# Graph attention on one core: query-key products added by plain products with the identity instead of by transposes and a selection matrix

## The chip, the core and the metric

The kernel runs on one core of a Trainium2 chip. A core has five engines that run side by side, each with its own queue of instructions that it takes in order: TensorE (PE, matrix products; its weight loads are shown apart as PEld), VectorE (DVE), ScalarE (ACT), GpSimd (POOL, which here mostly issues gathers) and SyncE (SP, which issues DMAs). Matrix products are written into PSUM, a small memory of eight banks of 512 float32 values on each of 128 partitions[...]. The metric is the time of one execution on the device in microseconds.

## What is computed

The input x is 8 batches of 2048 nodes with 256 features, and a 2048 x 2048 adjacency matrix that is nearly empty. Layer 0 is attention with 4 heads of 64 features, whose softmax runs over each chunk of 256 columns by itself; layer 1 is a graph attention over neighbours; each is followed by a residual and a layer norm. The part that matters here is the product of queries and keys:

```python
scores = jnp.einsum('bhnd,bhjcd->bhnjc', q, kc) / jnp.sqrt(jnp.asarray(Dh, dtype=q.dtype))
scores = jnp.clip(scores, -10.0, 10.0)
scores = jnp.where(mask == 0, jnp.asarray(-10.0, scores.dtype), scores)
attn = jax.nn.softmax(scores, axis=-1)
ctx = jnp.einsum('bhnjc,bhjcd->bhnd', attn, vc)
```

## The kernel before

The adjacency matrix has only a few neighbours in each row, so the kernel works on lists. `edge_lists` takes from each row the columns that are set, sorts the nodes by their number of neighbours and cuts them into 16 tiles of 128 nodes. All nodes of tile t are given the same number of slots, `CAPS[t]`, from 24 down to 5, together 164. A slot holds one neighbour of each of the tile's nodes.

The batches go in four groups of two (g = 0 to 3), so a row of keys has 512 values and there are 8 pairs of batch and head (`GH`). One step of layer 0 is one tile of one group, which makes 64 steps. The sequence is written out at the end of the function (L762 to L858): 32 steps of groups 0 and 1, then 32 steps of groups 2 and 3 with 16 steps of layer 1 (for the first four batches) put between them, then 16 steps of layer 1 alone. A scheduler may still move an instruction past others of its engine where no data forbids it, so that neighbouring steps mix on each engine.

In a step of layer 0 these functions run, in this order in the program:

- `fetch`, one step ahead (L802): `gather` (L483) has POOL fetch, slot by slot, the rows of keys and values of the neighbours into the tiles `u` of a ring. A tile `u` holds a unit, which is two slots (one where the number is odd and the unit is the last). It is released when TensorE has read it for the last time.
- `scores0` (L531): the products of queries and keys, told below.
- `rows1` (L653) for the step before the last and `finish0` (L629) for the last one: output projection, residual, layer norms and the table rows for layer 1.
- `tables` (L354), while g + 1 < 4: keys, values and queries of the next group, written to DRAM. So 48 of the 64 steps build tables.
- `softmax0` (L586): the clip, the exponential and the sums by chunk.
- `context0` (L610): VectorE (L501) or ScalarE (L507) multiplies the values by the weights, and TensorE adds the slots up (`summed`, L509) by transposes with the identity that accumulate in PSUM.

In `scores0` the 64 features of a head are split into 8 parts of 8: the columns of a row of keys are ordered (part j, batch and head, 8 features), 8 x 64 = 512. The first unit and the last third of the units are done by VectorE alone (`reduced`: multiply at L554, sum at L556). For the other units (`npe` - 1 of them: 8, 5, 5, 4, 4, 4, 4, 4, 4, 4, 3, 3, 3, 3, 2, 2 for the tiles, 62 in each group) VectorE only multiplies (`product`, L547), and writes the result over the keys of the unit before, sorted so that each part j has 128 columns, which are 2 slots x 8 pairs x 8 features. Then:

- TensorE transposes each of the 8 parts and adds them in PSUM (L566): the result in bank `pr` has the 128 columns on partitions and the 128 nodes along the row. Up to four units share the bank; there is one such bank.
- ScalarE copies the bank to `prT` in SBUF (L572, L574).
- TensorE multiplies each unit by `sel` (L576), a matrix of 128 x 16 that adds eight neighbouring partitions and so the last 8 features; the product has nodes on partitions again and is put in bank `tf`.
- In `softmax0` VectorE clips these scores on the way from `tf` to `sc` (L590) and those of the units that it summed itself (L593).

PSUM is full: `mf` 1 bank, `tk` 2, `acc` 2, `tf` 2, `pr` 1.

Of the kernel before, what the change touches and what calls it, by code (L numbers as in the profile page):

```python
# [9 lines left out]
F32 = mybir.dt.float32  # L10
# [4 lines left out]
ALU = mybir.AluOpType  # L15
AX = mybir.AxisListType

P = 128
H = 4
D = 64  # L20
DP = 8
NJ = D // DP
# [15 lines left out]
UNIT = 2  # L38
# [135 lines left out]
def sparse_path(ctx: ExitStack, tc: tile.TileContext, keep, x, adj, Wq, bq, Wk, bk, Wv, bv, Wo, bo, gamma, beta, W, a,  # L174
                out):
    nc = tc.nc
# [6 lines left out]
    GH = G * H  # L183
# [15 lines left out]
    const = ctx.enter_context(tc.tile_pool(name="const", bufs=1))  # L199
# [13 lines left out]
    def by_part(v):  # L213
        return v.rearrange("p (j h d) -> p h j d", h=H, d=DP)


    sel = const.tile([P, P // DP], F32, name="sel")
    nc.gpsimd.memset(sel, 1.0)
    nc.gpsimd.affine_select(out=sel, in_=sel, compare_op=ALU.is_ge, fill=0.0, base=0, pattern=[[-DP, P // DP]],
                            channel_multiplier=1)  # L220
    nc.gpsimd.affine_select(out=sel, in_=sel, compare_op=ALU.is_ge, fill=0.0, base=DP - 1, pattern=[[DP, P // DP]],
                            channel_multiplier=-1)
    biasT = const.tile([P, 3, KC], F32, name="biasT")

    def row(v):
# [6 lines left out]
    def bank(tag, bufs=2):  # L232

        return ps.tile([P, 512], F32, tag=tag, name=tag, bufs=bufs)
# [296 lines left out]
    def scores0(g, t):  # L531
        S = CAPS[t]
        qx, units = got0[g, t]
        q = qx[:, 0:GF]
        sc = small.tile([P, GH, S], F32, tag="sc", name="sc")

        npe = 1 + len(units) - len(units) // 3
        ps_sc = bank("tf")[:, 0:GH * S].rearrange("p (s e) -> p s e", e=GH)
        W8 = GH * DP
        qv = q.rearrange("p (k j w) -> p k j w", k=UNIT, w=W8).unsqueeze(3)  # L540

        def product(i):

            u, s0, n = units[i]
            room = units[i - 1][0][:, :, 0:GF]
            prod = room.rearrange("p k (j w) -> p k j w", w=UNIT * W8)[:, :, :, 0:n * W8]
            nc.vector.tensor_tensor(prod.rearrange("p k j (s w) -> p k j s w", w=W8),  # L547
                                    u[:, :, 0:GF].rearrange("p s (k j w) -> p k j s w", k=UNIT, w=W8),
                                    qv.to_broadcast([P, UNIT, NJ // UNIT, n, W8]), op=ALU.mult)
            return prod  # L550

        def reduced(u, s0, n):
            prod = u[:, :, 0:GF].rearrange("p s (j w) -> p s j w", w=W8)
            nc.vector.tensor_tensor(prod, prod, q.rearrange("p (j w) -> p j w", w=W8).unsqueeze(1)  # L554
                                    .to_broadcast([P, n, NJ, W8]), op=ALU.mult)
            nc.vector.tensor_reduce(sc[:, :, s0:s0 + n].rearrange("p e s -> p s e"),  # L556
                                    prod.rearrange("p s j (e d) -> p s e j d", d=DP),
                                    axis=AX.XY, op=ALU.add)
        reduced(*units[0])
        for i in range(1, npe, 4):  # L560
            some = units[i:min(i + 4, npe)]
            pr = bank("pr", 1).rearrange("p (k r) -> p k r", r=P)
            for k, (u, s0, n) in enumerate(some):
                prod = product(i + k)
                for j in range(NJ):
                    nc.tensor.matmul(pr[0:n * W8, k, :], prod[:, j // (NJ // UNIT), j % (NJ // UNIT), :], ident, is_transpose=True,  # L566
                                     start=(j == 0), stop=(j == NJ - 1), skip_group_check=True)
            m = len(some)
            prT = work.tile([P, 4, P], F32, tag="prT", name="prT", bufs=1)
            full = m - 1 if some[-1][2] < UNIT else m  # L570
            if full:
                nc.scalar.copy(prT[:, 0:full, :], pr[:, 0:full, :])  # L572
            if full < m:
                nc.scalar.copy(prT[0:W8, full, :], pr[0:W8, full, :])  # L574
            for k, (u, s0, n) in enumerate(some):
                nc.tensor.matmul(ps_sc[:, s0:s0 + n, :], prT[0:n * W8, k, :], sel[0:n * W8, 0:n * GH],  # L576
                                 start=(s0 == UNIT), stop=(k == m - 1 and i + m == npe), skip_group_check=True)
        for unit in units[npe:]:
            reduced(*unit)
        st0[g, t] = ps_sc, sc, min(S, UNIT * npe)  # L580


    ebuf = const.tile([P, GH * TOP + 1], F32, name="ebuf")
# [2 lines left out]
    def softmax0(g, t):  # L586
        S = CAPS[t]
        n = GH * S
        ps_sc, sc, sp = st0.pop((g, t))
        nc.vector.tensor_scalar(sc[:, :, UNIT:sp], ps_sc[:, UNIT:sp, :].rearrange("p s e -> p e s"), -10.0, 10.0, op0=ALU.max,  # L590
                                op1=ALU.min)
        for some in [sc[:, :, 0:UNIT]] + ([sc[:, :, sp:]] if sp < S else []):
            nc.vector.tensor_scalar(some, some, -10.0, 10.0, op0=ALU.max, op1=ALU.min)  # L593
        e = ebuf[:, 0:n]
        ev = e.rearrange("p (e s) -> p e s", s=S)
        nc.scalar.activation(ev, sc, AF.Exp)
# [56 lines left out]
    def rows1(g, t):  # L653

        o = st0.pop((g, t))
        pt = transposed(o.rearrange("p b f -> p (b f)"), "tf", 2)
        xT = work.tile([P, G * KC, P], F32, tag="x1T", name="x1T", bufs=1)
        nc.scalar.copy(xT, pt)  # L658
        wh = work.tile([P, WW], F32, tag="whs", name="whs")
# [627 lines left out]
```

## Time and profile before

| what | value |
|---|---|
| median of 3 runs | 2385.73 us (2379.63 to 2388.16) |
| the profiled execution | 2397.55 us, of which the span of instructions 2395.8 us |
| mean granted TensorE clock | 0.885 of full speed |
| score products on TensorE (L566) | 1984 instructions, from 223.6 to 1933.8 us |
| copies to prT on ScalarE (L572, L574) | 96 |
| gathers of keys and values on POOL (L489) | 656, mean 1235 ns |
| DMA engines | 279 GB/s, software queue 60.1% of the 16 engines' span |

All details come from the profiled execution. An engine is busy while at least one of its instructions is under way; matrix products overlap in TensorE's pipeline, and their ends are modelled, so its busy share is higher than the share in which it takes up new work. A line such as L566 is a line of the kernel before. A wait is put down to the instruction whose end came last. PE and PEld are the product and the weight load of the same unit; each product has its load.

### The profile page before, as it was taken

What the parts mean: (1) busy time and instruction counts of PE and PEld (TensorE: products, weight loads), DVE (VectorE), ACT (ScalarE), POOL (GpSimd) and SP (SyncE); (2) the same over time, 40 slices, a digit from 0 to 9 for tenths busy, and PEclk for the clock granted to TensorE, in tenths of its full rate; (3) what the DMA queues carried; (4) which work ended last, traced back from release to release, by engine and by line L of the source; (5) the groups of instructions that cost most, each with busy time, mean ns of one, the idle gap of its engine ahead of it and who ended that gap; (6) DMA issues with size and microseconds to landing.
All of it is one profiled execution on the core that took longest, in us unless ns stands there. A gap on an engine that the chain in (4) does not pass through costs nothing. (4 is left out here: it accounts for less than half of the span.)

```text
span 2395.8 us, 38844 instructions
## 1 busy us (share of the span) xinstructions
PE 1900.4 (79%) x11946; PEld 1622.0 (68%) x11946; DVE 1833.5 (77%) x4099; ACT 1409.0 (59%) x5036; POOL 1505.0 (63%) x1230
## 2 busy tenths in 40 slices
PE   7686889889899898999988885888678786664764
PEld 5565677778778787777876774776566675554653
DVE  6864587877588988588988886887788887775775
ACT  4573455546566555655565665664356677665766
POOL 3125455672666676376668856774677685787883
PEclk9897899899999999999998997987878987877887
DMA  7737877795889798598879977896679896786884
GB/s 259 242 137 272 265 270 281 260 346 209 316 287 320 260 334 319 212 388 298 302 258 353 360 281 238 285 321 221 230 274 326 306 319 248 278 310 231 302 296 154
DMA packets 239982, 669.10 MB, mean 279 GB/s; under 512 B 43688, under 2 KB 70059, under 8 KB 237719
## 3 DMA queue, kind: packets, MB, share of 16 engines
q0 software_dynamic: 156800, 505.01, 60.1%
q1 hardware_dynamic: 79248, 151.55, 17.2%
q10 hardware_dynamic: 3718, 9.97, 1.3%
q8 instruction: 98, 1.61, 0.3%
q14 instruction: 118, 0.96, 0.1%
HBM read 612.79 MB, written 126.36 MB: 309 GB/s over the span
## 5 line engine op out<-in xcount | busy, mean ns | idle before, releaser
L489 POOL DMA_INDIRECT u<-kv_d,idx x656 | 810.2, 1235 | 436.4 <-PE acc L514 185.7
L514 PE MATMUL acc<-ident,u 128*128 128x128 f32 x5248 | 713.4, 291 | 157.0 <-DVE u L501 89.0
L514 PEld LDWEIGHTS acc<-ident,u 128*128 128x128 f32 x5248 | 637.5, 151 | 220.7 <-DVE u L501 133.2
L489 POOL DMA_INDIRECT u<-wh_d,idx x328 | 416.5, 1270 | 148.2 <-issue 76.4
L566 PE MATMUL pr<-ident,u 128*128 128x128 f32 (+1 forms) x1984 | 287.0, 295 | 78.7 <-DVE u L547 77.2
L501 DVE TENSOR_TENSOR u<-u,al 128x1024 f32<-128x1024 f32 x280 | 334.5, 1234 | 1.5
L566 PEld LDWEIGHTS pr<-ident,u 128*128 128x128 f32 (+1 forms) x1984 | 245.4, 151 | 110.8 <-DVE u L547 104.6
L547 DVE TENSOR_TENSOR u<-u,qx 128x1024 f32<-128x1024 f32 (+1 forms) x248 | 302.0, 1218 | 18.3 <-DMA u<-kv_d,idx 15.1
L501 DVE TENSOR_TENSOR u<-u,z 128x1024 f32<-128x1024 f32 x266 | 314.4, 1212 | 0.6
L507 ACT ACTIVATE u<-u,z 128x64 f32<-128x64 f32 x1008 | 262.0, 337 | 25.0 <-DVE z L700 17.1
L507 ACT ACTIVATE u<-u,al 128x64 f32<-128x64 f32 x800 | 209.1, 342 | 23.2 <-DVE al L607 22.3
L663 PE MATMUL mf<-wa,x1T 128*128 128x264 f32 x512 | 167.6, 455 | 23.1 <-ACT x1T L658 14.8
L351 POOL TENSOR_TENSOR xt<-xt,beta_r 128x1024 f32<-128x1024 f32 x32 | 77.1, 2410 | 143.1 <-PE tk L336 126.3
L385 PE MATMUL tk<-wq,xT 128*128 128x256 f32 x512 | 145.2, 397 | 24.4 <-ACT kvs L379 24.4
L451 ACT ACTIVATE nm<-sums 128x2 f32<-128x2 f32 (+1 forms) x160 | 32.4, 202 | 221.3 <-DVE sums L641 122.6
L372 PE MATMUL tk<-wkv,xT 128*128 128x256 f32 x512 | 151.7, 410 | 12.9 <-ACT xC L341 12.6
L635 PE MATMUL mf<-wo,cT 128*128 128x256 f32 x512 | 148.4, 415 | 6.3 <-ACT whs L666 5.3
L376 PE MATMUL tk<-wkv,xC 128*128 128x256 f32 x512 | 144.5, 399 | 0.0
L663 PEld LDWEIGHTS mf<-wa,x1T 128*128 128x128 f32 x512 | 101.7, 218 | 59.7 <-ACT x1T L658 23.6
L455 ACT ACTIVATE sq<-o,nm 128x256 bf16<-128x256 f32 x256 | 129.7, 507 | 5.3
L554 DVE TENSOR_TENSOR u<-u,qx 128x1024 f32<-128x1024 f32 (+1 forms) x96 | 116.0, 1214 | 16.6 <-DMA qx<-qx_d,node 7.1
L590 DVE TENSOR_SCALAR sc<-tf 128x64 f32<-128x64 f32 (+5 forms) x64 | 14.0, 218 | 138.2 <-PE tf L576 138.2
(168 smaller groups left out, 3254.0 us busy)
## 6 DMA issues: line engine op xcount, KB each, us to landing
kv_d<-kvs SPq DMA_DIRECT2D x48, 512.0 KB, 6.0
wh_d<-whs SPq DMA_DIRECT2D x64, 260.0 KB, 5.8
xt<-in_x_dram SPq DMA_DIRECT2D x64, 256.0 KB, 4.8
qx_d<-xt SPq DMA_DIRECT2D x32, 512.0 KB, 4.4
qx_d<-qs SPq DMA_DIRECT2D x64, 256.0 KB, 5.8
x_d<-o SPq DMA_DIRECT2D x64, 256.0 KB, 5.2
xr<-x_d SPq DMA_DIRECT2D x32, 512.0 KB, 4.9
u<-kv_d,idx POOLq DMA_INDIRECT x656, 6.5
```

The costliest lines, as they stand in the source:

```text
L372: nc.tensor.matmul(pm[:, 0:F], xT[:, b * KC + kc, rows], wkv[:, kc, 0:F], start=(kc == 0), stop=False, skip_group_check=True)
L376: nc.tensor.matmul(pm[:, F:], xC[:, b * KC + kc, rows], wkv[:, kc, F:], start=False, stop=(kc == KC - 1), skip_group_check=True)
L385: nc.tensor.matmul(qb, xT[:, b * KC + kc, rows], wq[:, kc, :], start=(b == 0 and kc == 0), stop=False, skip_group_check=True)
L455: nc.scalar.activation(sq, src[:, k, :], AF.Square, bias=nm[:, k:k + 1], accum_out=m2[:, k:k + 1])
L489: nc.gpsimd.indirect_dma_start(out=u[:, k, 0:width], out_offset=None, in_=table, in_offset=bass.IndirectOffsetOnAxis(ap=idx[:, t, s0 + k:s ...
L501: nc.vector.tensor_tensor(pv, pv, av, op=ALU.mult)
L507: nc.scalar.activation(pe, pe, AF.Copy, scale=al[:, e, s0 + k:s0 + k + 1])
L514: nc.tensor.matmul(acc[:, c, :], part[:, k, c * P:(c + 1) * P], ident, is_transpose=True, start=first and k == 0 and c == 0, stop=last and ...
L547: nc.vector.tensor_tensor(prod.rearrange("p k j (s w) -> p k j s w", w=W8), u[:, :, 0:GF].rearrange("p s (k j w) -> p k j s w", k=UNIT, w=W8),
L566: nc.tensor.matmul(pr[0:n * W8, k, :], prod[:, j // (NJ // UNIT), j % (NJ // UNIT), :], ident, is_transpose=True, start=(j == 0), stop=(j ...
L635: nc.tensor.matmul(po[:, b, :], cT[:, b * KC + kc, :], wo[:, kc, :], start=(b == 0 and kc == 0), stop=False, skip_group_check=True)
L663: nc.tensor.matmul(pw[:, 0:F + 2 * H], xT[:, b * KC + kc, :], wa[:, kc, :], start=(kc == 0), stop=(kc == KC - 1))
```

## The change

A plain product with the identity as the stationary matrix gives back the moving matrix; eight of them into the same place in PSUM add eight matrices without transposing them. The change does this with the eight parts of a unit: the nodes stay on partitions, and the 128 columns of a unit (slots, pairs, 8 features) lie along the row of the bank. Four units fill a bank of 512. What is left, the sum over the last 8 features, is done by VectorE in `softmax0`, by a reduction that reads the bank. The copies to `prT`, the products with `sel` and `sel` itself go. The clip is one instruction over all of a tile's scores. Bank `pr` gets two buffers, `tf` keeps one, which only `rows1` uses.

```diff
@@ -213,13 +213,6 @@
-    sel = const.tile([P, P // DP], F32, name="sel")
-    nc.gpsimd.memset(sel, 1.0)
...
@@ -535,7 +528,7 @@
-        ps_sc = bank("tf")[:, 0:GH * S].rearrange("p (s e) -> p s e", e=GH)
+        sums = []
@@ -559,25 +552,18 @@
-            pr = bank("pr", 1).rearrange("p (k r) -> p k r", r=P)
+            ns = sum(n for _, _, n in some)
+            pr = bank("pr")
             for k, (u, s0, n) in enumerate(some):
                 prod = product(i + k)
+                part = pr[:, k * UNIT * W8:(k * UNIT + n) * W8]
                 for j in range(NJ):
-                    nc.tensor.matmul(pr[0:n * W8, k, :], prod[:, j // (NJ // UNIT), j % (NJ // UNIT), :], ident, is_transpose=True,
-                                     start=(j == 0), stop=(j == NJ - 1), skip_group_check=True)
-            m = len(some)
-            prT = work.tile([P, 4, P], F32, tag="prT", name="prT", bufs=1)
-            full = m - 1 if some[-1][2] < UNIT else m
-            if full:
-                nc.scalar.copy(prT[:, 0:full, :], pr[:, 0:full, :])
-            if full < m:
-                nc.scalar.copy(prT[0:W8, full, :], pr[0:W8, full, :])
-            for k, (u, s0, n) in enumerate(some):
-                nc.tensor.matmul(ps_sc[:, s0:s0 + n, :], prT[0:n * W8, k, :], sel[0:n * W8, 0:n * GH],
-                                 start=(s0 == UNIT), stop=(k == m - 1 and i + m == npe), skip_group_check=True)
+                    nc.tensor.matmul(part, ident, prod[:, j // (NJ // UNIT), j % (NJ // UNIT), :], start=(k == 0 and j == 0),
+                                     stop=(k == len(some) - 1 and j == NJ - 1), skip_group_check=True)
+            sums.append((some[0][1], ns, pr))
         for unit in units[npe:]:
             reduced(*unit)
-        st0[g, t] = ps_sc, sc, min(S, UNIT * npe)
+        st0[g, t] = sc, sums
@@ -586,11 +572,11 @@
-        ps_sc, sc, sp = st0.pop((g, t))
-        nc.vector.tensor_scalar(sc[:, :, UNIT:sp], ps_sc[:, UNIT:sp, :].rearrange("p s e -> p e s"), -10.0, 10.0, op0=ALU.max,
-                                op1=ALU.min)
-        for some in [sc[:, :, 0:UNIT]] + ([sc[:, :, sp:]] if sp < S else []):
-            nc.vector.tensor_scalar(some, some, -10.0, 10.0, op0=ALU.max, op1=ALU.min)
+        sc, sums = st0.pop((g, t))
+        for s0, ns, pr in sums:
+            nc.vector.tensor_reduce(sc[:, :, s0:s0 + ns].rearrange("p e s -> p s e"),
+                                    pr[:, 0:ns * GH * DP].rearrange("p (s e d) -> p s e d", e=GH, d=DP), axis=AX.X, op=ALU.add)
+        nc.vector.tensor_scalar(sc, sc, -10.0, 10.0, op0=ALU.max, op1=ALU.min)
@@ -653,7 +639,7 @@
-        pt = transposed(o.rearrange("p b f -> p (b f)"), "tf", 2)
+        pt = transposed(o.rearrange("p b f -> p (b f)"), "tf", 1)
```

More of the change, by code (lines that the diff above doesn't have):

```diff
@@ L214, in by_part @@
         return v.rearrange("p (j h d) -> p h j d", h=H, d=DP)
-    sel = const.tile([P, P // DP], F32, name="sel")
-    nc.gpsimd.memset(sel, 1.0)
[L219 to L222, printed above, removed]
     biasT = const.tile([P, 3, KC], F32, name="biasT")
```

## The prediction

> **What bounds the kernel now.** I read the page first (busy shares, slices, chain), then the busy time by stage, the groups with their shapes kept apart, the table of waits, and TensorE's timeline at one place. The chain of waits that the page prints holds only the last scatter, 0.1% of the span, so it says nothing about the middle; the stages have to. The steps that the change touches run from 230 us (first score) to 1940 us (last one); what comes before (edge lists) and after (layer 1 alone) is left as it is.
>
> ```profile
> PE 1900.4 (79%) x11946; PEld 1622.0 (68%) x11946; DVE 1833.5 (77%) x4099; ACT 1409.0 (59%) x5036; POOL 1505.0 (63%) x1230
> ...
> 230.00:780.00 550.00, 488.83 (x3045) 416.96 (x3046) 419.04 (x822) 296.20 (x1124) 322.07 (x261) 0.92 0.82 286
> 780.00:1250.00 470.00, 424.88 (x2809) 365.38 (x2808) 383.63 (x757) 278.23 (x1065) 303.84 (x237) 0.97 0.83 298
> 1250.00:1600.00 350.00, 283.38 (x1871) 245.37 (x1869) 282.54 (x623) 216.80 (x803) 254.43 (x196) 0.89 0.86 305
> 1600.00:1940.00 340.00, 256.49 (x1588) 219.24 (x1587) 275.04 (x598) 183.83 (x664) 231.36 (x183) 0.82 0.80 277
> ```
>
> Columns of the stages: length, then busy time and count of PE, its weight loads, DVE, ACT, POOL, then granted clock, DMA share, GB/s. While tables are built (the first two rows) PE is busy 89 and 90% of the time, DVE 76 and 82%; ACT and POOL have room. Later DVE is first (81%), PE second. So the two engines to which this change gives work are the two fullest ones, and the one that it relieves, ACT, is not.
>
> ```profile
> L566 PE MATMUL pr<-ident,u 128*128 128x128 f32 x1824 | 267.4, 296 | 78.7 <-DVE u L547 77.2
> L372 PE MATMUL tk<-wkv,xT 128*128 128x256 f32 x512 | 151.7, 410 | 12.9 <-ACT xC L341 12.6 <-ACT kvs L379 0.2
> L576 PE MATMUL tf<-sel,prT 128*128 128x16 f32 x456 | 65.7, 270 | 32.2 <-ACT prT L572 31.4
> L556 DVE TENSOR_REDUCE sc<-u 128x16 f32<-128x1024 f32 x84 | 101.8, 1212 | 0.5
> L738 DVE SCALAR_TENSOR_TENSOR xr<-mf,xr 128x512 f32<-128x512 f32 x64 | 43.8, 684 | 21.5 <-ACT hT L737 9.9 <-DMA xr<-x_d 7.5 <-SPq L868 4.1
> L572 ACT COPY prT<-pr 128x512 f32<-128x512 f32 x36 | 20.9, 581 | 33.2 <-PE pr L566 33.2
> ```
>
> Columns: line, engine, operation, output and input, shapes, count, then busy us and mean ns of one, then idle time before it and who ended it. The counts are the point here. L372 is a plain float32 matmul: the program issues 64 tables x 2 batches x 2 halves = 256 of them, the trace has 512 records. L566 is a transpose: 62 units x 4 groups x 8 = 1984 issued, and 1984 records (these 1824 and 160 of half width). A plain float32 product is two records, a transpose one.
>
> ```profile
> DVE sc L590 <- PE tf L576: 138.2, 54, 11.2
> DVE o L641 <- PE mf L313: 85.3, 35, 9.3
> PE pr L566 <- DVE u L547: 77.2, 52, 10.5
> ACT prT L572 <- PE pr L566: 54.6, 36, 7.3
> PE tf L576 <- ACT prT L572: 31.4, 22, 5.9
> ```
>
> Columns: who waited for whom, us in total, times, longest. VectorE's largest wait (138.2 us) is for the end of the scores at L590, 2.2 us for each of 64 steps. The same path holds ACT 54.6 us at the head of its queue and PE 31.4 us.
>
> ```profile
> 1209.82 1.03 PE L372 MATMUL tk<-wkv,xT 128*128 128x256 f32 x4
> 1210.68 0.38 PE L313 MATMUL tk<-ident,biasT 128*128 128x128 f32 x2
> 1210.90 1.03 PE L376 MATMUL tk<-wkv,xC 128*128 128x256 f32 x4
> 1211.77 0.59 PE L372 MATMUL tk<-wkv,xT 128*128 128x256 f32 x2
> ```
>
> Start to start, four records of 256 columns take 0.86 us (215 ns each, 0.84 ns per column), two transposes of 128 columns 0.22 us (110 ns each). The means in the groups (291 to 410 ns) contain pipeline latency; these spacings are the price of an issue.
>
> **What the Trainium skill says.** "FP8 and Floating Point Precision", TensorE Precision Notes: true float32 is four passes through the array. The trace agrees: two records at about 2 clocks of 2.4 GHz per column each. "TensorE: Matmul & The Clock Gate", Terms: the transpose mode is 4 times faster for float32; here, per column of output, 110 ns against 2 x 110 ns, so a factor of two. The same page, Back-to-back issue gap, says that the spacing is set by load and matmul together; here a 16-column product still costs what its load costs (the eight records of L576 at 1202.50 take 1.06 us with the last one's latency, about 115 ns each), and a 128-column transpose 110 ns with its load beside it.
>
> **The change part by part.** Everything is first summed against the profiled execution, 2397.55 us (span 2395.8).
>
> *Score products on TensorE.* 1984 transposes at 110 ns become 1984 plain products. With 128 columns each is two records of about 110 ns; in the 160 of half width 64 columns move, so two records of at best 55 ns, held up by the loads (115 ns): I count 0 to 20 us for them and take 10. Added: 1824 x 0.110 + 10 = 211 us of issue. That records of this kind overlap their loads follows from L372 (215 ns each with loads of some 200 ns beside them). Loading the same identity again costs a load per record, as the equal counts of PE and PEld show.
>
> *Selection products.* 496 records at 0.115 = 57 us of PE go. Net on PE: +154 us. Two thirds of the score records (673 + 624 of 1984) lie in the two table stages: +100 us there, on 1020 us in which PE is busy 914.
>
> *ACT copies.* 96 copies go, 41 us of ACT (36 x 581, 16 x 468, 12 x 364, 12 x 263, 20 x 254 ns). Worth nothing as busy time (59%), but two hops go with them: PE's 31.4 us of waiting, and ACT's standing at the head of its queue for 54.6 us while the table and row copies that PE wants wait behind it.
>
> *Reduction on VectorE.* 76 reductions read PSUM: 36 of 512 elements, 8 each of 448, 384, 320 and 128, 4 of 256 and 4 of 192. The trace has no reduction out of PSUM; it has a 512-element one-pass operation with a PSUM operand (684 ns) and a reduction of 1024 from SBUF (1212 ns). Both give about 0.15 us + 1.04 ns per element: 36 x 0.68 + 8 x (0.61 + 0.55 + 0.48 + 0.28) + 4 x (0.42 + 0.35) = 43 us; bounds 38 (no PSUM surcharge, half the fixed cost) and 50. Against it, the clip from PSUM (64, 14 us) and the small clips (84, 16 us) go, and one clip over all scores comes (64 x 0.21 = 13 us). Net +26 us of VectorE, bounds +20 and +33.
>
> *Order and buffers.* In the issue order of the two programs, counted per step between the first score product and the end of the scores, other work on PE's queue falls from 4.8, 4.7, 3.8, 2.1 us (four groups of 16 steps, priced by the spacings above) to 3.9, 3.3, 1.4, 2.5; the usual middle step has none. With no copy to wait for, scores stand in one block and tables, rows and the finish follow it. The block itself grows from 4.2 to 6.8 us. Bank pr now stays taken until VectorE's reduction, but it has two buffers, no tile needs more than two, and the next tile's products come after those reductions on VectorE anyway: 0. Bank tf with one buffer serves only rows1, once per step, its reader ACT done long before: 0. The set-up of sel on POOL (three instructions at the start) is worth nothing beside the lists. No DMA and no gather is moved; a gather waits for PE's context work (220.3 us in all), which gets later if PE does, and POOL at 63% absorbs that.
>
> *The tail of a step.* From the last product of a four-unit tile, before: 0.86 transposes, 0.27 latency, 0.63 copy, 1.06 selection, 0.26 clip = 3.1 us. After, with products at least 1.7 us apart: 1.76 + 0.27 + 0.68 + 0.21 = 2.9. With products back to back on VectorE (1.22 us each) PE falls behind by 0.54 us a unit, 1.6 us over the other three: 4.5. So the shorter chain pays only where VectorE has other work between products.
>
> *Sum.* Table stages: +100 on PE, less 22 of its waits for prT there, less 25 of the 35 us it waited for products (longer products fill them) = +53; neither engine paces alone, I take half: +27. VectorE's +26: half in the table stages (two thirds of it), all later: 9 + 9 = +18. Late tail: between -0.2 and +1.4 us a step, +0.2 x 23 = +5. Against it the freed ACT queue and the undivided score block, 0 to 1.2 us a step, 0.5 x 48 = -24. Together +26 us, 1.1%: 2397.55 becomes 2423.6, and at the ratio of the median to this execution (2385.73 / 2397.55 = 0.995) the forecast is 2411 us.
>
> **The rivals.** All at the median's scale; 0.5% (12 us) is about what a measurement of this kernel can tell from no change.
>
> *PE has room and the score path gets shorter: 2348.* For it: L590 is the largest wait of VectorE, ACT's blocked queue delays copies that PE needs, and its real issue load in the first stage is only about 420 of 550 us (its records at the spacings above). Then 1.2 us come off in each of 64 steps (77 us), less 26 for the reductions and some 13 of lag: -38. Against it: two records per product.
>
> *The two cancel: 2386.* The tail's 3.1 against 2.9 us speaks for it.
>
> *TensorE becomes the bound: 2500.* It is slower by one mechanism: in the 48 table steps PE's issue goes from about 18.3 to 20.5 us at full clock, 22.3 at 0.92, of a step of 23.9; from the point where PE no longer waits for anything there, all +100 count, with 26 of VectorE and 11 of late lag, less 22: +115. Against it: half of VectorE's waits would have to be PE's fault even now, and PE's own waits must not shrink.
>
> That the change doesn't do what it says I see no room for: the issue order shows the transposes and the selection gone.
>
> **How the numbers follow.** Slightly slower, 2411 (its own range 2398 to 2462): 0.44. PE the bound, 2500: 0.08. No change: 0.14. Faster, around 2348: 0.34. Slower by over 0.5% is thus 0.52, within 0.5% 0.14, faster 0.34. The range 2348 to 2462 leaves out about half of the faster case's lower part and the PE-bound case, together 0.2.
>
> **What would show it.** The score line should have about 3968 records, not 1984, at 110 ns spacing in a block; if it has 1984, PE gains 57 us and the forecast is wrong. The reduction should take 0.6 to 0.75 us for 512 elements. The wait of VectorE for the scores should stay near 2 us a step: if it falls below 1, the faster rival holds; if it passes 3.5 with PE above 95% in the table stages, PE is the bound. The stages before 230 us and the last 456 us should keep their lengths; a difference there would be none of the steps above.

## The result and the profile after

The changed kernel takes 2473.41 us (median of 4 runs, 2462.31 to 2477.99) where the kernel before takes 2382.68 (4 runs, 2378.05 to 2388.16): a ratio of 1.0373, 95% interval 1.033 to 1.0416. It is slower, as forecast, but by 91 us and not by 26. The lines below are from a profiled execution with a span of 2472.1 us.

The page's first part, busy time of each engine:

```profile
PE 1996.0 (81%) x13434; PEld 1766.9 (71%) x13434; DVE 1860.7 (75%) x4087; ACT 1371.3 (55%) x4940; POOL 1476.0 (60%) x1227
```

The groups of the changed kernel with shapes kept apart (line, engine, operation, shapes, count, then busy us and mean ns of one, then idle time before it and who ended it), and below them TensorE's timeline at one block of products (start us, length us, group; `tf` is the record that comes next):

```profile
L561 PE MATMUL pr<-u,ident 128*128 128x128 f32 x3648 | 463.3, 286 | 62.8 <-DVE u L540 61.6 <-PE tf L300 0.9
L561 PE MATMUL pr<-u,ident 128*128 128x64 f32 x320 | 39.0, 276 | 0.0
L577 DVE TENSOR_REDUCE sc<-pr 128x64 f32<-128x512 f32 x36 | 24.7, 686 | 24.5 <-PE pr L561 24.5
```

```profile
611.05 3.29 PE L561 MATMUL pr<-u,ident 128*128 128x128 f32 x28
614.17 0.49 PE L300 MATMUL tf<-ident,o 128*128 128x128 f32 x3
```

The prices came out much as forecast. The 1984 products are 3648 + 320 = 3968 records; 28 of them, back to back, take 614.17 - 611.05 = 3.12 us, 111 ns each. The 512-element reduction takes 0.686 us. Only the new clip is dearer, 20.5 us in all instead of 13, as three of its 64 instructions took 1.7 to 2.6 us. VectorE gained 27 us of busy time, ScalarE lost 38. So the prices are not where the forecast went wrong, and TensorE's busy share rose by two points only, to 81%.

Next, the stretches between the same steps of layer 0 in both kernels, cut at the sum by chunk in `softmax0` of the 11th, 32nd, 53rd and 64th step. Columns: stretch, its length, then busy time and count of PE, its weight loads, DVE, ACT, POOL, then granted clock, DMA share, GB/s. Before:

```profile
501.60:987.90 486.30, 442.90 (x2845) 380.19 (x2845) 384.99 (x783) 285.79 (x1118) 284.15 (x222) 0.96 0.80 286
987.90:1585.50 597.60, 508.09 (x3372) 437.95 (x3370) 483.32 (x1021) 362.71 (x1347) 421.46 (x329) 0.93 0.86 307
1585.50:1941.70 356.20, 270.22 (x1663) 230.82 (x1664) 287.17 (x627) 195.79 (x712) 242.82 (x192) 0.82 0.80 281
```

After:

```profile
496.90:1036.90 540.00, 489.30 (x3346) 436.06 (x3345) 394.09 (x789) 276.28 (x1095) 277.95 (x223) 0.97 0.73 263
1036.90:1683.50 646.60, 558.70 (x3855) 500.72 (x3853) 495.83 (x1024) 355.16 (x1322) 411.22 (x332) 0.93 0.80 286
1683.50:2011.30 327.80, 265.92 (x1924) 240.38 (x1924) 289.16 (x616) 186.43 (x684) 234.75 (x189) 0.93 0.85 300
```

The loss lies in the middle: 54 and 49 us over 42 steps, 37 of which build tables. The granted clock there is the same in both kernels (0.96 and 0.97, then 0.93 and 0.93), so it does not make this loss. The last 11 steps became 28 us shorter, but there the clock also rose, from 0.82 to 0.93. The steps before the 11th became 5 us shorter and layer 1 alone 7 us longer. In the first of these stretches PE is busy 489.30 of 540.00, 91%, and it was 442.90 of 486.30 before, also 91%. That does not decide between the rivals: a TensorE that is the bound would look like this, its busy time and the stretch growing together (by 46 and 54 us), and so would a kernel in which every engine waits longer.

The table of waits says what kind of time was added. (Who waited for whom, us in total, times, longest.) Before, four rows that the prediction did not show:

```profile
POOL u L489 <- PE acc L514: 220.3, 104, 16.9
...
DVE r L460 <- ACT y L458: 37.3, 27, 4.2
DVE ebuf L597 <- ACT ebuf L596: 23.9, 37, 3.6
...
DVE u L547 <- DMA u<-kv_d,idx: 15.1, 11, 2.6
```

After:

```profile
POOL u L482 <- PE acc L507: 317.9, 122, 14.8
...
DVE sc L577 <- PE pr L561: 92.2, 44, 9.7
...
DVE r L453 <- ACT y L451: 65.6, 38, 9.7
DVE u L540 <- DMA u<-kv_d,idx: 59.2, 32, 6.9
DVE ebuf L583 <- ACT ebuf L582: 46.6, 40, 5.2
DVE o L627 <- PE mf L306: 40.3, 17, 12.2
```

Two waits of VectorE fell: the one for the scores, from 138.2 to 92.2 us, and the one for the output projection, from 85.3 to 40.3. Read alone, they promise a faster kernel. Three rose: at the products for the gathered keys (+44), in the row norms for ScalarE (+28), in the softmax for the exponential (+23). That is 95 us, 4 more than the two gave, and 27 us of busy time come on top; the rest of the 76 us by which the span grew is spread over smaller rows. And POOL waits 98 us longer for a unit of the ring to come free, and ScalarE 69 us longer for the row transposes (`x1T`: 90.2 us, 21.4 before). So the waits moved from one set of places to another, which is what a new order of the work looks like; whether it is that, or only TensorE's price seen elsewhere, the profile alone cannot tell.

### The profile page after: what moved, and what is told of

It reads as the page before. It is cut to its first block, busy times and chain, and to the rows that moved or that the text cites. A ratio compares the mean times of both kernels' runs of the same rounds, so it can differ in the third digit from the quotient of the medians.

```text
span 2472.1 us, 41629 instructions
## 1 busy us (share of the span) xinstructions
PE 1996.0 (81%) x13434; PEld 1766.9 (71%) x13434; DVE 1860.7 (75%) x4087; ACT 1371.3 (55%) x4940; POOL 1476.0 (60%) x1227
## 5 line engine op out<-in xcount | busy, mean ns | idle before, releaser
L482 POOL DMA_INDIRECT u<-kv_d,idx x656 | 789.2, 1203 | 488.9 <-PE acc L507 237.2
L507 PE MATMUL acc<-ident,u 128*128 128x128 f32 x5248 | 694.8, 289 | 153.5 <-DVE u L494 83.5
L507 PEld LDWEIGHTS acc<-ident,u 128*128 128x128 f32 x5248 | 623.5, 149 | 206.7 <-DVE u L494 120.4
L561 PE MATMUL pr<-u,ident 128*128 128x128 f32 (+1 forms) x3968 | 499.0, 285 | 62.8 <-DVE u L540 61.6
L561 PEld LDWEIGHTS pr<-u,ident 128*128 128x128 f32 x3968 | 483.0, 201 | 74.2 <-DVE u L540 72.4
L540 DVE TENSOR_TENSOR u<-u,qx 128x1024 f32<-128x1024 f32 (+1 forms) x248 | 291.7, 1176 | 64.3 <-DMA u<-kv_d,idx 59.2
L649 PE MATMUL mf<-wa,x1T 128*128 128x264 f32 x512 | 157.5, 433 | 39.9 <-ACT x1T L644 23.5
L649 PEld LDWEIGHTS mf<-wa,x1T 128*128 128x128 f32 x512 | 94.9, 205 | 78.6 <-ACT x1T L644 36.3
L621 PE MATMUL mf<-wo,cT 128*128 128x256 f32 x512 | 139.1, 395 | 12.1 <-ACT whs L652 10.8
L547 DVE TENSOR_TENSOR u<-u,qx 128x1024 f32<-128x1024 f32 (+1 forms) x96 | 112.6, 1176 | 31.9 <-DMA qx<-qx_d,node 17.7
L378 PEld LDWEIGHTS tk<-wq,xT 128*128 128x128 f32 x512 | 94.5, 198 | 40.6 <-ACT kvs L372 30.4
```

The costliest lines, as they stand in the source:

```text
L378: nc.tensor.matmul(qb, xT[:, b * KC + kc, rows], wq[:, kc, :], start=(b == 0 and kc == 0), stop=False, skip_group_check=True)
L482: nc.gpsimd.indirect_dma_start(out=u[:, k, 0:width], out_offset=None, in_=table, in_offset=bass.IndirectOffsetOnAxis(ap=idx[:, t, s0 + k:s ...
L507: nc.tensor.matmul(acc[:, c, :], part[:, k, c * P:(c + 1) * P], ident, is_transpose=True, start=first and k == 0 and c == 0, stop=last and ...
L561: nc.tensor.matmul(part, ident, prod[:, j // (NJ // UNIT), j % (NJ // UNIT), :], start=(k == 0 and j == 0), stop=(k == len(some) - 1 and j ...
L621: nc.tensor.matmul(po[:, b, :], cT[:, b * KC + kc, :], wo[:, kc, :], start=(b == 0 and kc == 0), stop=False, skip_group_check=True)
L649: nc.tensor.matmul(pw[:, 0:F + 2 * H], xT[:, b * KC + kc, :], wa[:, kc, :], start=(kc == 0), stop=(kc == KC - 1))
```

## The experiments

Two theories stand against each other at first. *Price*: the two records for each product occupy TensorE for longer, and that is the loss. *Order*: the scheduler, which decides from its own prices what goes ahead of what on each engine, made another order for the changed kernel, and that order is worse. The runs came from several chips with different times for the kernel before (2384 to 2589 us), so only ratios to the kernel before on the same chip are compared; that such a ratio carries over to another chip is assumed. Waits in us are compared only among runs on chips where it takes 2383 to 2388 us.

### One part of the change at a time

**Plain products alone.** The kernel before, whose copies, selection and clips stay, with the transposes of L566 made plain products.

```diff
-  nc.tensor.matmul(pr[0:n * W8, k, :], prod[...], ident, is_transpose=True, ...)
+  nc.tensor.matmul(pr[0:n * W8, k, :], prod[...], ident, ...)
```

> The kernel before, in which the 1984 transposes of the products become plain products with the same operands (the result is the same matrix); copies, selection, banks and VectorE stay as they were. Theory 1 (TensorE's doubled records are the loss, and in the table stages nearly all of it counts): all of the added issue and none of the saved selection, so at least as slow as the changed kernel, 2470 to 2550 us, with 3968 records at L566. Theory 2 (the loss comes from the reductions on VectorE, the later finish in the order, and the banks): 2380 to 2410 us, since none of these is in this kernel.

Measured: 1.0644 [1.0557, 1.0732]. The plain products, with the order that comes with them, cost more than the whole change; what the change takes away (copies, selection) may give part of it back.

**Half the products.** The changed kernel, adding parts 0 to 3 of 8 on TensorE only; the other four are left out.

```diff
-  for j in range(NJ):
+  for j in range(NJ // 2):
```

> The changed kernel with only the first 4 of the 8 parts of each unit added on TensorE; the other half of each score's sum is left out, so the record count of the score line is 1984, as many as the transposes had. VectorE's work and all waits keep their form. Theory 1: TensorE then has 57 us less to issue than before the change, so 2340 to 2400 us. Theory 2: 2440 us or more.

Measured: 0.9885 [0.9829, 0.9942], below the kernel before. With 992 products fewer (at 2 x 111 ns, 220 us of issue) some 4.7 points come off the changed kernel's ratio. It looks like a proof of the price theory. It isn't one, because the scheduler made a new order for this kernel too.

**No reduction.** The changed kernel with a copy of the first of the eight features in place of the sum over them; the other seven are left out of the score.

```diff
-  nc.vector.tensor_reduce(sc[...], pr[...], axis=AX.X, op=ALU.add)
+  nc.vector.tensor_copy(sc[...], pr[...][:, :, :, 0])
```

> The changed kernel in which VectorE copies the first of the last 8 features out of the bank instead of adding the eight; that sum is left out. 76 operations of 64 elements at most instead of 512: about 29 us less of VectorE, the same waits. Theory 1: VectorE isn't what paces the table stages, so 2450 to 2475 us. Theory 2 (VectorE's work counts in full): 2430 to 2447 us.

Measured: 1.0321 [1.0247, 1.0395], not told apart from the changed kernel's 1.0373. VectorE's new work does not show as a large part of the loss.

**The change in the last group only.** The kernel before for groups 0 to 2, the changed way for group 3, whose steps build no tables, with the sums in banks `pr` and `tf`.

```diff
+  plain = g == NG - 1
...
+  if plain:
+      pr = bank("tf") if sums else bank("pr", 1)
+      nc.tensor.matmul(part, ident, prod[...], ...)
```

> The kernel before for groups 0 to 2 (48 steps, which build tables) and the changed way for group 3 (16 steps without tables); the second bank of a tile is one of tf. In the changed kernel the steps 48 to 63 took about 22 us less than before the change. Theory 1 (plain products cost only where TensorE is full, and elsewhere the shorter path gains): 2350 to 2373 us, faster than both. Theory 2 (the shorter last group was only work that had been late and was caught up, or chance): 2377 to 2395 us.

Measured: 1.0107 [1.0042, 1.0172]. I had hoped that this would beat both kernels, since the last steps had become shorter. It doesn't: the gain does not come along with the steps.

**Both kernels again**, unaltered, beside the next runs.

> The kernel before once more, so that its trace comes from the same chip as the runs beside it. Every theory: within 0.5% of the other runs of it there.

> The changed kernel once more, beside the runs of this call. Every theory: 3 to 4.2% above the kernel before on the same chip.

Measured: the kernel before has a span of 2395.1 us again, with 143.6 us of waiting for the scores (138.2 in the first profile) and 14.4 for the gathered keys (15.1); but POOL's row at the ring is 241.2 us instead of 220.3. The changed kernel: 1.0355 [1.0326, 1.0384], with 95.5 and 50.0 us (92.2 and 59.2 in its first profile) and 328.3 at the ring. So most rows are good to some 10 us, the one at the ring to some 20. The ratio 1.0355 is the one that the runs below are held against.

**TensorE relieved elsewhere.** The 512 bias products in `tables` left out (the biases, which are zero in the data, are thus not added), once in the changed kernel and once in the kernel before.

```diff
-  add_bias(pm[:, 0:F], biasT[:, 1])
...
-  add_bias(qb, biasT[:, 0])
```

> The changed kernel without adding the biases of keys and queries in the tables (they are zero in these inputs); left out are 512 transposes, of which 384 lie in the 48 table steps: 384 x 0.110 = 42 us of TensorE, nothing of any other engine. Theory 1 (TensorE paces the table steps, and most of what it issues there counts): 29 to 42 us less than the changed kernel. Theory 2 (half or less of it counts, as the forecast took): 8 to 21 us less.

> The kernel before without the same 512 transposes, 42 us of TensorE in the 48 table steps. If TensorE paced these steps before the change too, 29 to 42 us less than before (ratio 0.982 to 0.988). If it only came to pace them by the change, 0 to 21 us less (0.991 to 1.0).

Measured: the changed kernel goes to 1.0009 [0.9988, 1.0029], 83 us less for at most 512 x 0.11 = 56 us of TensorE. The kernel before goes to 1.0106 [1.008, 1.0133]: it does *less* work and takes 25 to 29 us *more* (by the ratio and by the medians). Read by the price alone, both are odd. But two other things moved. Both kernels had been ordered anew, as their traces show, so an edit of the source that the scheduler sees changes two things at once; this spoils the reading of the four runs above. And the granted clock moved: 0.916 in the changed kernel without the biases (0.912 with them), 0.875 in the kernel before without them (0.889 with them, the median on this chip). In these traces the clock stands at full or at half speed, so a mean of 0.875 over 2417 us is half speed for some 600 us, against some 530 before. Half of the difference, some 35 us, is the most that TensorE can lose by it (an estimate), and that is more than the loss. In the changed kernel the same estimate gives at most 15 to 20 us, and 83 less that is not far from the 56 us taken away. So these two runs do not show what an order is worth; the first of them rather says that TensorE's work counts in the changed kernel.

### Order and price taken apart

From here the operands or the kind of the product instructions were altered after the scheduler had made its order. Then every engine issues the same list in the same places (where the same order was traced twice, the sequences agree), and the price of those instructions is the one thing that was changed. The granted clock is not held by this, so it is given with the runs.

**The order of before, the price of plain products.** The result is the same matrix.

```diff
+  # after the order is made
+        new = [_copy.replace(i, is_transpose=False) if ...
+               and str(i.outs[0].memref).rsplit("/", 1)[-1].startswith("pr_") else i for i in ins]
```

> The kernel before in exactly its own order on every engine, but the 1984 transposes of the products are turned into plain products after the order was made (same result): only TensorE's price changes, by 211 us of issue. Theory 1 (the price on TensorE is the loss): ratio 1.05 to 1.08, as where the order was made anew (1.064). Theory 2 (most of it is the new order that the scheduler makes from its own prices): 1.00 to 1.03.

Measured: 1.0517 [1.0422, 1.0612]. The waits of this run:

```profile
POOL u L489 <- PE acc L514: 313.8, 119, 16.2
DVE sc L590 <- PE tf L576: 261.2, 57, 11.4
```

The price shows here: 1984 x 0.11 = 218 us of issue cost 123 us, although the granted clock rose (0.917; the median of the kernel before on this chip is 0.889). Among VectorE's waits it stands in one row, that for the scores: 261.2 against 138.2 us, 123 us more.

**The order made for plain products, the price of transposes.** The reverse: the first experiment's order, with transposes put back.

> The reverse: the order that the scheduler made for plain products in the kernel before, but the products are turned back into transposes after it. The same instructions at the same prices as the kernel before, in another order. Theory 1: 0.99 to 1.01. Theory 2: 1.03 to 1.06.

Measured: 1.0533 [1.0434, 1.0632]. These are the instructions of the kernel before, at its prices, in another order, and it costs as much as the price did, 127 us. The granted clock is lower, 0.870 instead of 0.889, which is half speed for some 650 us instead of 530. At most half of these 120 us can be lost by it (an estimate), so at least some 65 us are the order's own. VectorE's waits:

```profile
DVE sc L590 <- PE tf L576: 114.5, 43, 11.4
DVE z L680 <- DMA u<-wh_d,idx: 91.1, 46, 6.5
DVE r L460 <- ACT y L458: 76.4, 42, 9.1
DVE u L547 <- DMA u<-kv_d,idx: 66.2, 34, 5.5
```

This is the pattern of the changed kernel: a smaller wait for the scores, and larger ones for the row norms (76.4; 65.6 there; 37.3 before) and for the gathered keys (66.2; 59.2; 15.1). It has come here without the change and without its price, so at least the rows for the gathered keys belong to the order; the row norms rose to 54.9 with the price alone, in the run above. And in this order the price is worth little: 1.0644 with it, 1.0533 without, two intervals that overlap, though from two chips.

**The changed kernel in the order made for transposes.** The scheduler was shown transposes, and plain products were put in afterwards.

> The instructions of the changed kernel, in the order that the scheduler makes when it takes the products for transposes; they are turned into plain products after it. The same prices as the changed kernel, in another order. Theory 1: 1.027 to 1.047, within 1% of the changed kernel (1.037). Theory 2: off it by more than 1%, on either side.

Measured: 1.044 [1.0346, 1.0534]. The wait for the gathered keys falls to 26.1 us, that for the scores rises to 201.2. Another order, no better; the two are not told apart.

**The changed kernel's own order, cheap products.** Nothing moved; the products and the identity are read as the upper 2 bytes of each value, so what is added is cut to 8 significant bits.

```diff
+  # after the order is made
+            if ... str(i.outs[0].memref).rsplit("/", 1)[-1].startswith("pr_"):
+                i = _copy.replace(i, ins=[_copy.replace(v, dtype=_mybir.dt.bfloat16, offset=2 * v.offset + 1, ...) for v in i.ins])
```

> The changed kernel with every instruction in its place on every engine; only the 1984 instructions that add the products read the upper half of each 4-byte word as a 2-byte number (for the products and for the identity), so that what is added are products cut to 8 significant bits; PE is expected to leave one record instead of two for each. If each costs at most the 110 ns of one record, PE loses at least 1824 x 0.110 = 200 us. Theory price (the loss of the changed kernel is PE's longer occupation): the time falls below that of the kernel before, to a ratio of 0.97 to 1.0, and DVE's wait for pr falls from 92 us to under 50. Theory order (the loss is the new order, in which context, row and norm work come after an undivided score block): the ratio stays at 1.02 to 1.036, DVE's wait for pr falls, but POOL's wait at the ring (318 us), ACT's at x1T (90) and DVE's for the gather (59) stay within 20% of where they are.

Measured: 1.0306 [1.0256, 1.0357]. The page's first part, and two blocks from TensorE's timeline:

```profile
PE 1796.4 (73%) x11450; PEld 1509.9 (61%) x11450; DVE 1861.1 (75%) x4087; ACT 1371.1 (56%) x4940; POOL 1484.6 (60%) x1227
```

```profile
1137.09 1.09 PE L561 MATMUL pr<-u,ident 128*128 128x128 bf16 x16
1138.48 0.63 PE L561 MATMUL pr<-u,ident 128*128 128x128 bf16 x8 [0.30 <-DVE u L540]
```

A product is now one record, and (1.09 - 0.63) / 8 gives 57 ns for it instead of 222. So 1984 x 0.165 = 327 us of issue at full clock are gone, more than the change had added, and 200 us of PE's busy time with them. The ratio falls from 1.0355 to 1.0306, half a per cent or some 12 us. Its waits:

```profile
POOL u L482 <- PE acc L507: 304.2, 112, 14.7
...
DVE r L453 <- ACT y L451: 73.3, 37, 8.2
DVE o L627 <- PE mf L306: 70.9, 30, 10.0
...
DVE u L540 <- DMA u<-kv_d,idx: 63.6, 37, 6.4
```

VectorE's wait for the sums has nearly gone (16.6 us), but the freed time turns up at the projection (70.9, was 40.3) and at the exponential (74.0, was 46.6), while the ring, the norms and the gathered keys stay about as they were. ScalarE's wait for the row transposes, which I expected to stay, fell from 90.2 to 40.2.

This looks like the run that decides, against the price. It does not, because the granted clock fell with the price: 0.844 here, 0.912 in the changed kernel, which is half speed for some 770 instead of some 430 us. Below are the steps 12 to 32 (the changed kernel had 540.00, 489.30 of PE and 0.97 there), and TensorE at a place at half speed (first two lines) and at full speed (last two):

```profile
500.10:1036.30 536.20, 423.19 (x2722) 353.87 (x2721) 393.81 (x787) 277.52 (x1095) 271.66 (x219) 0.89 0.73 261
```

```profile
1074.55 1.06 PE L378 MATMUL tk<-wq,xT 128*128 128x256 f32 x2
1075.41 0.63 PE L300 MATMUL tf<-ident,o 128*128 128x128 f32 x2
...
1080.62 1.03 PE L378 MATMUL tk<-wq,xT 128*128 128x256 f32 x4
1081.48 0.87 PE L649 MATMUL mf<-wa,x1T 128*128 128x264 f32 x3
```

TensorE is busy for 79% of this stretch instead of 91%, and the stretch is as long. But what it still has to do is slower in part: in 0.86 us it starts two records of the table products at half speed and four at full speed. As the order is the same on every engine, the steps of the two kernels can be laid side by side (for the changed kernel the mean of its two traces). Of the 63 intervals from one sum by chunk to the next, 20 have less than 2 us of half speed more than in the changed kernel; they are 1.3 us shorter on average. The other 43 are 0.5 us longer on average. Even two executions of one and the same kernel differ in this way, by 0.33 to 0.45 us of length for each us of half speed. So at an unchanged clock the cheap products would give some 63 x 1.3 = 82 us (an estimate), and the clock took that back. The run shows that cheaper products alone do not make this kernel fast; it does not show that the order hides their price.

**Cheap products that the scheduler knows of.** VectorE rounds each product to 2 bytes as it writes it; the identity is a 2-byte copy.

```diff
-  room = units[i - 1][0][:, :, 0:GF]
+  room = units[i - 1][0].bitcast(BF16)[:, :, 0:GF]
...
-  nc.tensor.matmul(part, ident, prod[...], ...)
+  nc.tensor.matmul(part, identh, prod[...], ...)
```

> The changed kernel in which VectorE rounds each product to a 2-byte number as it writes it, and the identity is a 2-byte copy, so that the scheduler knows the cheaper price and makes its order from it. What is computed differs in the rounding of each product. PE loses at least 200 us against the changed kernel. Theory price: ratio 0.96 to 1.0 to the kernel before. Theory order: anything between 0.96 and 1.03, with the waits of the changed kernel where the order is still that of an undivided score block. If VectorE writes 2-byte products at another price than 4-byte ones, its share moves: 1095 us of products either way is the number to look at.

Measured: 1.014 [1.0094, 1.0186], with 22.5 us of waiting for gathered keys. Better than the changed kernel, and still behind the kernel before, although TensorE has less to do than in either; the granted clock is low here too, 0.848.

**The banks of before.** The changed kernel with one bank for the sums and two for the row transposes.

```diff
-  pr = bank("pr")
+  pr = bank("pr", 1)
...
-  pt = transposed(..., "tf", 1)
+  pt = transposed(..., "tf", 2)
```

> The changed kernel with the PSUM banks shared out as before: one bank for the sums (pr) instead of two, two for the row transposes (tf) instead of one. Theory banks: the single tf bank is why ACT waits for x1T (90 us, 21 before); with two that wait falls under 40 us and the ratio under 1.025. Theory order: the transposes come late because the rows come late, not for want of a bank; the ratio stays at 1.03 to 1.05, and with one pr bank DVE's wait for the sums does not fall below 92 us.

Measured: 1.0365 [1.0291, 1.0438]. The banks are worth nothing that can be measured.

**Full price in an order made for cheap products.** The changed kernel's arithmetic; the scheduler was shown 2-byte products, and the 4-byte operands were put back afterwards.

> The arithmetic of the changed kernel, with its full price (1984 instructions of two records each), in the order that the scheduler makes when it takes them for the cheap 2-byte ones: the operands are put back to 4 bytes after the order is made. Theory price: at least the changed kernel's 1.036. Theory order: the changed kernel's own order is a bad draw, and this one, near that of the run with 2-byte products (1.014), gives 1.014 to 1.03, with POOL's wait at the ring under 280 us (318 in the changed kernel) and DVE's waits for the gather at its products under 40 us (59), while its wait for pr rises over 92 us.

Measured: 1.0773 [1.0707, 1.0839], the slowest of all. My expectation of 1.014 to 1.03 was wrong, and so was its premise that the changed kernel's order is merely a bad draw. Against the run with 2-byte products (1.014) the price costs about 6% here, if the two chips, 2384 and 2589 us for the kernel before, can be compared.

### What the pairs say together

| order made for | at the cheaper price | at the full price | the price costs |
|---|---|---|---|
| transposes (kernel before) | 1 | 1.0517 | 5.2% |
| 2-byte products | 1.014 | 1.0773 | 6.2% |
| plain products (kernel before with its copies) | 1.0533 | 1.0644 | 1.1%, intervals overlap |
| plain products (changed kernel) | 1.0306 | 1.0355 | 0.5%, intervals overlap |

(In the second row the sequences in the two traces agree, but for one copy of the identity on VectorE.) In the end result, an order made with the full price in mind shows little of it, and an order made without pays 5 to 6%. Two things stand beside this table. Its second and third rows compare runs on different chips. And the granted clock of the profiled executions differs within each row: 0.885 and 0.917, 0.848 and 0.866, 0.870 and 0.876, 0.844 and 0.912. So the 0.5% of the last row is the price less what the lower clock took back, and how much the order itself hides is not shown. The run of the changed kernel in the order made for transposes (1.044) has no partner at a cheaper price.

The two orders made for plain products are 3 and 5% behind the kernel before even when the products are cheap, at the lower clock that came with them. They share one mark in the trace. VectorE's wait for gathered keys at the products (L540 or L547) is 41 to 66 us in every run, on whatever chip, whose order was made for plain 4-byte products in full number and in all groups, and 14 to 26 us in all others. My reading is that the scheduler takes the products up early, nearer to the arrival of the gathers, so that TensorE has time for them, and that what waits behind them on VectorE's queue is late. But the mark is not the loss: the changed kernel without the biases has it (41.4 us) and is as fast as the kernel before, and the changed kernel in the order made for transposes lacks it (26.1 us) and is at 1.044. Which trait of an order costs the time stays open.

## Why the prediction was right or wrong

*Records and prices: right.* 3968 records at 111 ns, the reduction at 0.686 us, VectorE +27 us (+26 forecast), ScalarE -38 (-41), the stretch before the first score unchanged, layer 1 alone 7 us longer. "FP8 and Floating Point Precision", TensorE Precision Notes in the Trainium skill, counts four passes for true float32; the trace after the change agrees as before, with 2 x 111 ns for 128 columns. The factor between transpose and plain product is two here, as read from the trace before, not four.

*The direction: right, by luck.* Forecast were +27 for TensorE's price, +18 for VectorE, +5 for the late tail and -24 for the order. The sum is positive because the price and VectorE's work were entered as costs, but neither TensorE's term nor that for the order has the right size. For the reduction the runs give about 8 us (1.0355 to 1.0321, not told apart from zero). For the price in the changed kernel they give 12 us with the lower clock and some 82 at an unchanged one (an estimate), for more issue than the change had added. How the rest of the 91 us divides between price and order stays open. The clock, which the forecast left as it was, does not explain the loss: it rose, from 0.885 to 0.913.

*The step that failed* is the one on order and buffers, with its term "the freed ACT queue and the undivided score block, 0 to 1.2 us a step, 0.5 x 48 = -24". I counted how much other work falls between the first product and the end of the scores, saw that the block stood undivided, and counted that as a gain. It was bounded on one side only: a block that stands together also stands in front of something. I did not ask what moved behind it. The runs show no gain in its place: VectorE's wait for the scores fell by 46 us and that for the projection by 45, and three others rose by 95; and in the kernel before, an order made for plain products costs 5.3% by itself, of which at least some 65 us are not the clock's. The same step says "No DMA and no gather is moved" and lets POOL absorb later releases. The gathers of keys and values kept their order, but those of the queries and of layer 1 stand at other places among them in POOL's queue, POOL's wait at the ring grew by 98 us and VectorE's for their data by 44.

*The half for TensorE* ("neither engine paces alone, I take half: +27") failed as well. It was a guess at how much of a net +53 shows, and it has no single answer: 0.5% in an order planned for it, with a lower clock in the comparison, and 5.2% in the order of before. It was reckoned for a kernel in which nothing is re-ordered, and there 123 of 218 us of added issue show. Part of the reckoning was a misreading: tables are built beyond the first two rows of stages, until 1423 us, so more than two thirds of the score products meet them; and from 1250 to 1600 us VectorE is not the fullest engine, PE is as full (283.38 and 282.54 us).

*The sign to look for misled.* I wrote that a score wait below 1 us a step would show the faster rival. It fell from 2.2 to 1.4, short of that sign, and the kernel became slower; with cheap products it fell to 0.3, and the kernel was still 3% slower than before. The wait tells how long VectorE stands at the scores, not what is lost elsewhere for it.

*The rivals.* TensorE as the bound, at 2500, is nearest in number, and its mechanism is not ruled out: PE is busy for 91% of the steps 12 to 32, and 83 us went when 56 us of its work were left out, though in a new order. Against it stands that with 327 us of issue taken away the time hardly moves, at a lower clock. Faster, at 2348, had the right observation, a shorter path to the scores, without its cost. Banks counted at 0: right. That removing the copies and the selection is a gain fits the runs (1.0644 with them, 1.0355 without, VectorE's new work included), though the orders and the chips differ.

## What to carry to other kernels

Where a scheduler sets the order, the price of an instruction and the order made from that price are two changes; take them apart by altering the instruction after the order is made, before any edit of the source is read as the cost of one part. A wait that shrinks on the path that was changed is no gain until the waits that grew elsewhere have been added up. An order that changes has to be priced with both signs: in this kernel the same instructions at the same prices differ by 5% between two orders, and the clock explains at most half of that. And the granted clock belongs into every such comparison: making TensorE's products cheaper came with a fall from 0.912 to 0.844, and that alone can turn the reading of an experiment round.

## What was not expected of the chip and the order

- The same instructions at the same prices in two orders: 1 and 1.0533 [1.0434, 1.0632]. Less work in another order: 1.0106 [1.008, 1.0133] with 512 products fewer, a loss that the lower clock can explain.
- With cheaper products on TensorE and the same order on every engine, the granted clock fell from 0.912 to 0.844. At the place shown at half speed TensorE had waited 5.76 us just before; whether such idle time brings the clock down was not tested.
- At full clock the accumulating product with the identity costs 57 ns for 128 columns of 2-byte operands, 2 x 111 ns for 4-byte ones, and the transpose of 4-byte values 110 ns.
- VectorE gained nothing from writing 2-byte products: the same multiplication of 1024 elements takes 1199 ns either way, as the two rows show, of the run with 2-byte products and of the changed kernel in its second set of runs:

```profile
L542 DVE TENSOR_TENSOR u<-u,qx 128x1024 bf16<-128x1024 f32 (+1 forms) x248 | 297.4, 1199 | 24.9 <-DMA u<-kv_d,idx 22.5 <-DVE u L496 0.7
```

```profile
L540 DVE TENSOR_TENSOR u<-u,qx 128x1024 f32<-128x1024 f32 (+1 forms) x248 | 297.4, 1199 | 58.3 <-DMA u<-kv_d,idx 50.0 <-PE pr L561 5.8 <-DVE z L680 0.8
```

No version that I tried with the whole computation beats the kernel before.
